# A gated attention layer whose output projection takes seven products: one group's token sums and another group's output products take other places in the order

## The chip, the cores and the metric

The kernel runs on one core of a Trainium2 chip. The metric is the device time of one execution in microseconds (us); lower is better. Several runs are made and their median is taken.

Five engines work side by side, each on its own queue of instructions, in the order in which the program has put them: TensorE (PE in the profile, PEld for its weight loads), VectorE (DVE), ScalarE (ACT), GpSimd (POOL) and SyncE (SP), which here only issues DMAs. Engines wait for one another through semaphores.

## What is computed

`x` and `ctx` are 64 x 128 x 512 in float32; all products are in float32. Cut to what matters:

```python
def xattn(x, k, v):                      # 4 heads of 128
    Q, K, V = heads(x) @ Wh, heads(k) @ Wh, heads(v) @ Wh
    masked = (Q K^T / sqrt(128)) * decay
    A = maximum(abs(masked.sum(over the batch)), 1)     # one A for all 64 sequences
    Y = layernorm(A @ V) * gamma + beta
    return (relu(x @ wg) * Y) @ wo

def ffn(x):                              # inner width 1408
    return ((silu(x @ gate.T * gate_s) * (x @ up.T * up_s)) @ down.T) * down_s

x = x + tanh(g_xattn) * xattn(layernorm(x), ctx, ctx)
x = x + tanh(g_ffn) * ffn(layernorm(x))
```

`A` needs the scores of all 64 sequences, so there are two passes: the first computes the scores and the gates `relu(x @ wg)`, the second everything else.

## The kernel before, in words

The 64 sequences are worked on in 16 groups of four (512 tokens). Products by `wg`, `wo`, `gate`, `up` and `down` are done as products of halves with seven products instead of eight; the price is sums of weights, made once, and sums of tokens, made for each group.

**First pass** (L637 to L670, a loop over groups). For group g:

- `prepare` (L522): for each of the four sequences, statistics on VectorE (`bn`, L251, with two instructions: bn_stats and an aggregate), `inv_std` (L245: an addition `ve` on VectorE, then a power on GpSimd, L249), the normalised tokens `xn` on VectorE (L281), a transpose `pt` on TensorE through an identity (L260), and a copy of `pt` to `xnT`, on VectorE (L552) for odd sequences and on ScalarE (L554) for even ones. For g = 0 the power is made for each sequence by itself, for later groups once for four.
- `scores` (L558) of the group before: products `pq` and `sv`, copies by ScalarE, and additions to `attn` on VectorE (L592, L594).
- `project` (L597) of the group before: first the four token sums `t` of `combine_b` (L322) on VectorE, each of 128 x 512 from the tile `xnT`; then the seven products into the banks a, f, b and c of PSUM, each of four matmuls of 128 x 256, with copies and sums between them.

`gate_weights` (L378) makes the four sums of the `wg` halves on GpSimd, once, when group 1 is prepared. `sum_wo` (L413) scales `down_s` (`ds`, `minus_ds`) and `wo` (`wo_raw`) on VectorE and makes the sums of `wo` on GpSimd; `prepare_weights` (L489) runs it as the first of the weight preparations that are spread over the groups.

**Second pass** (from L676 on). For each group: `retention` (L697) computes `A @ V` (products `po`), statistics and the product with the gate; `attended` (L768) computes the output projection in seven products (`wo_product`, L777) into the tiles bx, bz and by, adds them to `x_t` (L791), and then makes the second layernorm; `ffn` (L912) does the rest. `attended` first makes four sums `ys` (`combine_a`, L328), then yields after each product. While `ffn` of one group runs, `retention` and `attended` of later groups are woven into it: `interleave` (L100) takes steps of several generators in turn, in proportion to the number of steps that it is told for each. For the second group (g = 1) the attention runs beside `ffn` of group 0, in `late_attended` (L1110), which yields nine times, takes the sums, yields three times more and then goes through the products.

**What sets the order.** The program is traced in the order of the Python code, and a scheduler then orders the instructions of each engine by priority and readiness. `tc.issue_after(ins)` puts the instructions of its block behind `ins` where both are on the same engine. The kernel keeps such marks in small lists: `last_norm` (the last `xn`), `last_copy` (the last VectorE copy of `pt`), `last_product` (the last matmul of a `product`, L289), `last_down` (the last matmul of the down projection, L1062). In the version before, the statistics of group 1 are put behind the last copy of group 0, those of later groups behind the last `xn` (L644), and the first output product of a group is put behind the last matmul of the down projection, or behind the last `product` where there was none (L800).

Of the kernel before, what the change touches and what calls it, by code (L numbers as in the profile page):

```python
# [12 lines left out]
ALU = mybir.AluOpType  # L13
# [13 lines left out]
DB11, DB21, DB22, DT1, DT2, DT3, DT4 = range(7)  # L27
# [99 lines left out]
def flamingo_gated_layer(  # L127
# [21 lines left out]
    nc = tc.nc  # L149
    P = 128  # L150
    B, S, DIM = x.shape
# [5 lines left out]
    NG = B // GB  # L157
# [16 lines left out]
    ps_mm = ctx.enter_context(tc.tile_pool(name="ps_mm", bufs=3, space=PSUM))  # L174
    ps_bank = ctx.enter_context(tc.tile_pool(name="ps_bank", bufs=1, space=PSUM))

    last_ve, last_copy = [None], [None]
    last_load, last_norm, last_power, last_product = [None], [None], [None], [None]
    last_down, mid_down = [None], [None]

# [57 lines left out]
    for seeded in (bank_b, bank_c0, bank_c1):  # L238
        for i in range(TOK // P):
            last_seed = nc.tensor.matmul(  # L240
                seeded[:, i * P : (i + 1) * P], lhsT=ident, rhs=ident,
                start=(i == 0), stop=True, skip_group_check=True,
# [79 lines left out]
    def combine_b(engine, t, b11, b12, b21, b22):  # L322
        for dst, in0, in1 in (
            (t[0], b12, b11), (t[1], b22, t[0]), (t[2], b22, b12), (t[3], b21, t[1]),
        ):
            engine.tensor_tensor(dst, in0, in1, ALU.subtract)

    def combine_a(engine, s, a11, a12, a21, a22):  # L328
        engine.tensor_tensor(s[0], a21, a22, ALU.add)
# [34 lines left out]
    tanh_g = const.tile([P, 2], F32, name="tanh_g")  # L364
# [5 lines left out]
    for h in range(H):  # L370
        with tc.issue_after(last_seed.ins):
            nc.tensor.matmul(
                pg[:, h, :], lhsT=whT_sb[:, h, :], rhs=whT_sb[:, h, :],
                start=True, stop=True,
# [37 lines left out]

    def sum_wo(raw):  # L413

        nc.vector.tensor_scalar_mul(ds, ds, tanh_g[:, 1:2])
        nc.vector.tensor_scalar_mul(minus_ds, ds, -1.0)
        nc.vector.tensor_scalar_mul(raw, raw, tanh_g[:, 0:1])
        t = once.tile([P, 4, KC, HN], F32, tag="sums", name="wo_t")
        b = (
            raw[:, 0:KC, 0:HN], raw[:, 0:KC, HN:DIM], raw[:, KC:NC, 0:HN], raw[:, KC:NC, HN:DIM],  # L420
        )
        combine_b(nc.gpsimd, [t[:, i] for i in range(4)], *b)
        return [
            (wo_scr[m], src)
            for m, src in zip(range(7), (b[0], b[2], b[3], t[:, 0], t[:, 1], t[:, 2], t[:, 3]))
        ]
# [95 lines left out]
    def prepare(g, x_t, xnT):  # L522

        n = GB if g else 1

        def statistics(j):
            bn(mean_var[:, g * GB + j, :], x_t[j // 2][:, j % 2, :])
            if (j + 1) % n == 0:
                cols = slice(g * GB + j + 1 - n, g * GB + j + 1)
                inv_std(rstd[:, cols], mean_var[:, cols, 1], LN_EPS, n)  # L530

        def next_statistics(j):

            if g == 0 and j < GB:
                with tc.issue_after((last_norm[0] or last_ve[0]).ins):
                    statistics(j)

        for j in range(1 if g == 0 else GB):
            statistics(j)
        next_statistics(1)  # L540
        yield
        for j in range(GB):
            b = g * GB + j
            with ExitStack() as order:
                if g == 0:
                    order.enter_context(tc.issue_after(last_ve[0].ins))
                xn = normalised(
                    x_t[j // 2][:, j % 2, :], mean_var[:, b, 0:1], rstd[:, b : b + 1]
                )
            pt = transposed(xn, "pt")  # L550
            if j % 2:
                last_copy[0] = nc.vector.tensor_copy(xnT[:, :, j * S : (j + 1) * S], pt)  # L552
            else:
                nc.scalar.copy(xnT[:, :, j * S : (j + 1) * S], pt)  # L554
            next_statistics(j + 2)
            yield
# [40 lines left out]
    def project(g, xnT):  # L597

        b11, b12, b21, b22 = as_b(xnT)
        t = once.tile([P, 4, KC, HT], F32, tag="t1", name="t1")  # L600
        combine_b(nc.vector, [t[:, i] for i in range(4)], b11, b12, b21, b22)
        w = once.tile([P, 2, 2, TOK], F32, tag="w1", name="w1")
        m5 = att.tile([P, TOK], F32, tag="m1", name="m5p")
        bank_c = bank_c0
        product(bank_a, wgc[:, GA11], b11, True)
        nc.scalar.copy(bank_c, bank_a)
        yield
        product(bank_f, wgc[:, GS1], t[:, 0], True)
        nc.scalar.copy(m5, bank_f)
        yield  # L610
        product(bank_a, wgc[:, GA12], b21, False)
        nc.scalar.activation(w[:, 0, 0, :], bank_a, AF.Relu)
        yield
        product(bank_c, wgc[:, GS2], t[:, 1], False)
        nc.scalar.copy(bank_b, bank_c)
        yield
        product(bank_c, wgc[:, GS3], t[:, 2], False)
        nc.vector.tensor_add(w[:, 1, 1, :], bank_c, m5)
        yield
        product(bank_b, wgc[:, GS4], b22, False)  # L620
        nc.vector.tensor_add(w[:, 1, 0, :], bank_b, m5)
        nc.scalar.activation(w[:, 1], w[:, 1], AF.Relu)
        yield
        product(bank_c, wgc[:, GA22], t[:, 3], False)
        relu = nc.scalar.activation(w[:, 0, 1, :], bank_c, AF.Relu)
        if g == NG - 1:

            with tc.issue_after(relu.ins):
                sil = stat.tile([P, 1], F32, tag="rs", name="first_sil")
                nc.scalar.activation(sil, zeros[:, 0:1], AF.Silu)  # L630
        for q in range(2):
            nc.scalar.dma_start(out=w_scr[g, q], in_=w[:, q])
        yield

    pending = None
    weights = prepare_weights()
    first_power = [None]  # L637
    for g in range(NG):
        x_t, c_t = x_next.pop(0), c_next
        xnT = wide.tile([P, NC, TOK], F32, tag="xT", name="xnT")  # L640
        prep = prepare(g, x_t, xnT)
        if g:

            with tc.issue_after((last_copy if g == 1 else last_norm)[0].ins):  # L644
                next(prep)
        else:
            next(prep)
        if g == 1:

            with tc.issue_after(first_power[0].ins):  # L650
                gate_weights()
            constants()
        elif g > 1:

            with tc.issue_after(last_load[0].ins), tc.issue_after(last_power[0].ins):
                next(weights, None)
        held = project(pending[0], pending[2]) if pending else None

        steps = 0 if g == NG - 1 else 7
        interleave(  # L660
            (prep, GB),
            (scores(*pending) if pending else None, 2 + H),
            (islice(held, steps) if pending and steps else None, steps),
        )
        x_next.append(load_x((g + 2) % NG))
        if g + 1 < NG:
            c_next = load_ctx(g + 1)
        pending = (g, c_t, xnT)
        if g == 0:
            first_power[0] = last_power[0]  # L670
# [97 lines left out]
    def attended(g, x_t, ws, x1nT):  # L768
# [6 lines left out]
        yield  # L775

        def wo_product(bank, m, lhs, start):  # L777
            w = att.tile([P, KC, HN], F32, tag="wo", name="wo_w", bufs=3)
            nc.sync.dma_start(out=w, in_=wo_scr[m])
            for i in range(2):  # L780
                for k in range(KC):
                    nc.tensor.matmul(  # L782
                        bank[:, i * HN : (i + 1) * HN],
                        lhsT=lhs[:, k, i * P : (i + 1) * P],
                        rhs=w[:, k, :],
                        start=(start and i == 0 and k == 0),
                        stop=(i == 1 and k == KC - 1),
                        skip_group_check=True,
                    )
# [4 lines left out]

        d1, d2 = slice(0, HN), slice(HN, DIM)
        bx = ps_mm.tile([P, TOK], F32, tag="mm", name="bx")
        if g == 0:
            wo_product(bx, DB11, a11, True)
        else:
            with tc.issue_after((last_down[0] or last_product[0]).ins):  # L800
                wo_product(bx, DB11, a11, True)
        m1 = att.tile([P, TOK], F32, tag="m1", name="m1")
        nc.scalar.copy(m1, bx)  # L803
        for q, d in ((0, d2), (1, d2), (1, d1)):
# [305 lines left out]
    def late_attended(g, x_t, x1nT):  # L1110
        for _ in range(9):
            yield
        steps = attended(g, x_t, ws, x1nT)
        next(steps)
        for _ in range(3):
            yield
        yield from steps

    pending = (0, x_t, x1nT, combine_tokens(nc.vector, x1nT))
    for g in range(NG - 1):  # L1120
        x_t = x_next.pop(0)
        x1nT = new_x1nT()
        if g + 2 < NG:
            x_next.append(load_x(g + 2))
        steps = [attended(g + 1, x_t, ws, x1nT)] if g else [second]
        n_steps = ATT_STEPS + RET_STEPS
        if g == 0:
            steps.append(late_attended(1, x_t, x1nT))
            n_steps += RET_STEPS - 4 + 5
        if g + 2 < NG:  # L1130
            steps.append(next_retention(g + 2))
        interleave(
            (ffn(*pending), FFN_STEPS), (chain(*steps), int(n_steps * 1.4)),
        )
        with tc.issue_after(mid_down[0].ins):
            tokens = combine_tokens(nc.vector, x1nT)
        pending = (g + 1, x_t, x1nT, tokens)
# [59 lines left out]
```

## Time and profile before

| | |
|---|---|
| median of 3 runs | 2223.5 us (2223.39 to 2224.55) |
| the profiled execution | 2223.54 us |
| its span, from the first to the last instruction in the trace | 2221.7 us |
| TensorE busy | 2210.0 us (99%) |
| VectorE, ScalarE, GpSimd busy | 53%, 29%, 29% |
| TensorE clock granted | 1.00 on average |
| first pass | up to about 376 us |

The idle times of TensorE can be counted on two hands, in us from the start of the span: 1.82 ahead of the first matmul, 1.16 at 7.8 and 0.93 at 9.6 (group 0's transposes), 0.57 at 17.2, 0.84 at 19.7, 0.23 at 401, 0.10 at 416, 0.55 at 422, 0.57 at 425, 1.55 at 463, 0.32 at 500, and 3.0 behind the last matmul.

How to read it: a line of a timeline gives the start, the time taken, the engine, the line of the program, the operation, what it writes and what it reads, the shape and how many such instructions are merged. An idle time of the engine just ahead of it stands in brackets with what ended it. A matmul of the program shows as two or more of the profile's records, and their ends are modelled, so a product's length is better taken from one start to the next. A line of a table of stretches gives the stretch, its length, then the busy time of TensorE, its weight loads, VectorE, ScalarE and GpSimd, then the granted TensorE clock (1.00 is full), the share of time in which the DMA engines were busy, and GB/s. The page names the line where a helper issues an instruction, so L326 is any token sum and L281 any normalised tile.

### The profile page before, as it was taken

How to read it: one execution, taken by the hardware profiler on the slowest of the kernel's cores; microseconds unless marked ns; L12 is line 12 of the kernel's file. 1: busy time of each engine (PE TensorE's matmuls, PEld its weight loads, DVE VectorE, ACT ScalarE, POOL GpSimd, SP SyncE). 2: the span in 40 equal slices, each digit the busy share in tenths (PEclk: the TensorE clock that was granted, in tenths of full speed). 3: DMA queues.
4: the chain of work that ended last, by engine and by line, in shares of the span. 5: the costliest groups of instructions: out<-in, count | busy, mean ns of one | idle time of the engine just before them, and what ended most of it. 6: DMA issues, size and time to landing. Idle time of an engine off the chain costs nothing.

```text
span 2221.7 us, 28775 instructions
## 1 busy us (share of the span) xinstructions
PE 2210.0 (99%) x10112; PEld 1889.1 (85%) x10112; DVE 1176.9 (53%) x2866; ACT 642.8 (29%) x1242; POOL 646.3 (29%) x1007
## 2 busy tenths in 40 slices
PE   9999999999999999999999999999999999999999
PEld 7878887788888888888888888888888888888888
DVE  6445554656555555554546464636464646464624
ACT  3444444332222222222222222222222222231221
POOL 2223530241323232323233333333333323241020
PEclk9999999999999999999999999999999999999999
DMA  9886776678686878786878777787777777766654
GB/s 307 268 302 248 259 256 236 242 236 291 242 284 225 285 235 273 236 275 234 274 240 271 250 259 262 251 268 245 261 244 264 244 265 245 268 224 233 229 180 146
DMA packets 217104, 558.47 MB, mean 251 GB/s; under 512 B 21120, under 2 KB 63616, under 8 KB 200192
## 3 DMA queue, kind: packets, MB, share of 16 engines
q1 hardware_dynamic: 211536, 539.58, 72.3%
q10 hardware_dynamic: 5424, 17.04, 1.9%
q8 instruction: 81, 1.33, 0.2%
q14 instruction: 63, 0.52, 0.1%
HBM read 454.31 MB, written 102.24 MB: 251 GB/s over the span
## 4 chain that ended last, share of the span: by engine, by line
PE 98%; DVE 1%; DMA 0%; POOL 0%; issue 0%; ACT 0%; SPq 0%; ACTq 0%; POOLq 0%
PE bank_c L289 22%; PE bank_a L289 15%; PE bank_c L1062 9%; PE bank_b L289 7%; PE bank_f L289 7%; PE bank_b L1062 6%; PE sv L578 5%; PE bank_a L1062 4%; PE bank_f L1062 4%; PE by L782 4%; PE bz L782 3%; PE pq L563 2%; PE bx L782 2%; PE po L704 2%; PE bank_c L942 2%; PE pt L260 1%
## 5 line engine op out<-in xcount | busy, mean ns | idle before, releaser
L289 PE MATMUL bank_c<-tcomb,gu 128*128 128x256 f32 x1920 | 455.0, 380 | 0.3 <-DVE ve L248 0.3
L289 PEld LDWEIGHTS bank_c<-tcomb,gu 128*128 128x128 f32 x1920 | 363.3, 190 | 59.2 <-issue 7.2
L337 POOL TENSOR_TENSOR h<-h 128x128 f32<-128x128 f32 x540 | 243.5, 480 | 400.4 <-DVE h L932 284.2
L289 PE MATMUL bank_a<-x1nT,gu 128*128 128x256 f32 x1280 | 303.1, 379 | 0.6 <-ACT sil L957 0.6
L289 PEld LDWEIGHTS bank_a<-x1nT,gu 128*128 128x128 f32 x1280 | 242.4, 190 | 46.7 <-issue 13.4
L1062 PE MATMUL bank_c<-dn_w,h 128*128 128x256 f32 x896 | 212.0, 379 | 0.0
L1062 PEld LDWEIGHTS bank_c<-dn_w,h 128*128 128x128 f32 x896 | 170.1, 190 | 23.5 <-ACT bank_c L1042 0.2
L931 ACT ACTIVATE sil<-c,gs_sb 128x256 f32<-128x256 f32 x176 | 89.4, 508 | 332.1 <-DVE c L1021 172.3
L337 DVE TENSOR_TENSOR h<-h 128x128 f32<-128x128 f32 x644 | 161.1, 307 | 4.6
L1021 DVE TENSOR_TENSOR c<-bank_c,m 128x512 f32<-128x512 f32 x80 | 55.2, 690 | 202.1 <-PE bank_c L289 200.7
L793 POOL TENSOR_TENSOR x_t<-x_t,m 128x512 f32<-128x512 f32 x48 | 62.1, 1322 | 344.4 <-ACT m L803 320.8
L763 POOL TENSOR_TENSOR w_t<-w_t,yT 128x256 f32<-128x256 f32 x108 | 88.8, 853 | 243.1 <-ACT yT L754 243.1
L249 POOL TENSOR_TENSOR rs<-ve,mhalf 128x1 f32<-128x1 f32 x128 | 73.4, 585 | 294.1 <-DVE ve L248 224.8
L1062 PE MATMUL bank_b<-dn_w,h 128*128 128x256 f32 x640 | 156.4, 379 | 0.0
L289 PE MATMUL bank_f<-tcomb,gu 128*128 128x256 f32 x640 | 151.2, 379 | 0.0
L289 PE MATMUL bank_b<-x1nT,gu 128*128 128x256 f32 x640 | 151.2, 379 | 0.0
L289 PEld LDWEIGHTS bank_b<-x1nT,gu 128*128 128x128 f32 x640 | 121.6, 190 | 22.1 <-issue 6.2
L289 PEld LDWEIGHTS bank_f<-tcomb,gu 128*128 128x128 f32 x640 | 121.6, 190 | 16.5
L1062 PEld LDWEIGHTS bank_b<-dn_w,h 128*128 128x128 f32 x640 | 121.6, 190 | 16.5
L1082 DVE TENSOR_TENSOR x_t<-x_t,bank_c 128x256 f32<-128x256 f32 x192 | 77.7, 419 | 87.4 <-PE bank_c L1062 87.4
L951 ACT COPY bank_c<-bank_a 128x256 f32<-128x256 f32 x16 | 5.7, 357 | 400.2 <-PE bank_a L942 400.2
L578 PE MATMUL sv<-qw,c_t 128*128 128x256 f32 x512 | 120.5, 379 | 0.0
(153 smaller groups left out, 3362.7 us busy)
## 6 DMA issues: line engine op xcount, KB each, us to landing
dn_w<-dn_scr SPq DMA_DIRECT2D x320, 384.0 KB, 4.9
gu<-gu_scr SPq DMA_DIRECT2D x80, 1024.0 KB, 7.8
gu<-gu_scr SPq DMA_DIRECT2D x80, 768.0 KB, 6.2
x_t<-in_x_dram SPq DMA_DIRECT2D x62, 512.0 KB, 5.7
sq_scr<-sq SPq DMA_DIRECT2D x30, 1024.0 KB, 4.8
wo_w<-wo_scr SPq DMA_DIRECT2D x112, 256.0 KB, 3.8
dn_w<-dn_scr SPq DMA_DIRECT2D x96, 256.0 KB, 5.0
c_t<-in_ctxT_dram SPq DMA_DIRECT2D x64, 256.0 KB, 5.9
```

The costliest lines, as they stand in the source:

```text
L249: last_power[0] = nc.gpsimd.tensor_tensor(dst, ve, mhalf[:, :n], ALU.pow)
L289: last_product[0] = nc.tensor.matmul(out, lhsT=w[:, s, k, :], rhs=x_k, start=(start and s == 0 and k == 0), stop=(s == 1 and k == KC - 1), ...
L337: engine.tensor_tensor(slots[to], slots[a], slots[b], ALU.add if sign == "+" else ALU.subtract)
L563: nc.tensor.matmul(pq, lhsT=gram[:, h, :], rhs=xnT[:, h, :], start=True, stop=True)
L578: nc.tensor.matmul(sv[:, 0 : 2 + i : 1 + i, :], lhsT=c_t[j][:, h, :], rhs=qw[:, h, j : GB + 1 : GB - j, :], start=(i == 0), stop=(i == 1), ...
L763: (helper if d or g == 1 else nc.gpsimd).tensor_tensor(w, w, yT[:, :, d * KC + k, q * 2 : q * 2 + 2, :], ALU.mult)
L782: nc.tensor.matmul(bank[:, i * HN : (i + 1) * HN], lhsT=lhs[:, k, i * P : (i + 1) * P], rhs=w[:, k, :], start=(start and i == 0 and k == 0 ...
L793: engine.tensor_tensor(dst, dst, src.rearrange("p (b d) -> p b d", b=2), ALU.add)
L931: nc.scalar.activation(sil, gate, AF.Silu, scale=gs_sb[:, i : i + 1])
L1021: nc.vector.tensor_add(c22, bank_c, m5)
L1062: last_down[0] = nc.tensor.matmul(places[acc], lhsT=hq[q][:, a, :], rhs=dn[n][:, q, :], start=start, stop=True, skip_group_check=True,)
L1082: add = nc.vector.tensor_tensor(dst, dst, places[acc], ALU.add if sign > 0 else ALU.subtract)
```

## The change

In the first pass, for g = 1, `project` of group 0 is started (`next(held)`) before `prepare` of group 1 takes its first step, so that the token sums and the first product are traced first; and the statistics of group 1 are put behind the last of these sums instead of behind the last copy. `combine_b` returns its last instruction for that. The three VectorE instructions of `sum_wo` are put behind the last `xn`.

In the second pass every output product of groups after the first is put behind the last `product` matmul, where before only the first one of a group was put behind the last matmul of the down projection. `late_attended` yields five times instead of three between the sums and the second part, and the number of steps told to `interleave` grows by four.

```diff
-    last_ve, last_copy = [None], [None]
+    last_ve, last_sum = [None], [None]
...
@@ combine_b
-            engine.tensor_tensor(dst, in0, in1, ALU.subtract)
+            last = engine.tensor_tensor(dst, in0, in1, ALU.subtract)
+        return last
...
@@ sum_wo
-        nc.vector.tensor_scalar_mul(ds, ds, tanh_g[:, 1:2])
-        nc.vector.tensor_scalar_mul(minus_ds, ds, -1.0)
-        nc.vector.tensor_scalar_mul(raw, raw, tanh_g[:, 0:1])
+        with tc.issue_after(last_norm[0].ins):
+            nc.vector.tensor_scalar_mul(ds, ds, tanh_g[:, 1:2])
+            nc.vector.tensor_scalar_mul(minus_ds, ds, -1.0)
+            nc.vector.tensor_scalar_mul(raw, raw, tanh_g[:, 0:1])
...
@@ prepare
-                last_copy[0] = nc.vector.tensor_copy(xnT[:, :, j * S : (j + 1) * S], pt)
+                nc.vector.tensor_copy(xnT[:, :, j * S : (j + 1) * S], pt)
...
@@ project
-        combine_b(nc.vector, [t[:, i] for i in range(4)], b11, b12, b21, b22)
+        last_sum[0] = combine_b(nc.vector, [t[:, i] for i in range(4)], b11, b12, b21, b22)
...
@@ the loop of the first pass
         prep = prepare(g, x_t, xnT)
+        held = project(pending[0], pending[2]) if pending else None
+
+        steps = 0 if g == NG - 1 else 7
+        if g == 1:
+
+            next(held)
+            steps -= 1
         if g:
 
-            with tc.issue_after((last_copy if g == 1 else last_norm)[0].ins):
+            with tc.issue_after((last_sum if g == 1 else last_norm)[0].ins):
                 next(prep)
...
-        held = project(pending[0], pending[2]) if pending else None
-
-        steps = 0 if g == NG - 1 else 7
...
@@ attended
         def wo_product(bank, m, lhs, start):
+            if g:
+
+                with tc.issue_after(last_product[0].ins):
+                    return wo_matmuls(bank, m, lhs, start)
+            return wo_matmuls(bank, m, lhs, start)
+
+        def wo_matmuls(bank, m, lhs, start):
             w = att.tile([P, KC, HN], F32, tag="wo", name="wo_w", bufs=3)
...
-        if g == 0:
-            wo_product(bx, DB11, a11, True)
-        else:
-            with tc.issue_after((last_down[0] or last_product[0]).ins):
-                wo_product(bx, DB11, a11, True)
+        wo_product(bx, DB11, a11, True)
...
@@ late_attended
-        for _ in range(3):
+        for _ in range(5):
             yield
...
@@ the loop of the second pass
-            n_steps += RET_STEPS - 4 + 5
+            n_steps += RET_STEPS - 4 + 9
```

## The prediction

> **What bounds the kernel now.** I read the page first (engines' busy shares, chain that ended last), then who waited for whom on TensorE, then the timelines of TensorE, VectorE and GpSimd at the two places the change touches.
>
> ```profile
> PE 2210.0 (99%) x10112; PEld 1889.1 (85%) x10112; DVE 1176.9 (53%) x2866; ACT 642.8 (29%) x1242; POOL 646.3 (29%) x1007
> ...
> PE 98%; DVE 1%; DMA 0%; POOL 0%; issue 0%; ACT 0%; SPq 0%; ACTq 0%; POOLq 0%
> ```
>
> TensorE (PE) is busy 2210.0 of 2221.7 us. The change removes no matmul, so it can give back only part of the 11.7 us of idle time. About 3.0 of those lie behind the last matmul and 1.8 ahead of the first. The waits, longest first (us in total, times, longest):
>
> ```profile
> PE pt L260 <- DVE xn L281: 2.9, 3, 1.2
> ...
> PE bz L782 <- DVE ys L329: 1.6, 1, 1.6
> PE bank_f L289 <- DVE mean_var L254: 0.6, 1, 0.6
> ...
> PE bank_c L289 <- DVE ve L248: 0.3, 1, 0.3
> ```
>
> The first edit aims at the third line and part of the first (0.57 and 0.84 us near 18 and 20 us), the second at the lines of bz and bank_c (1.55 us at 463, 0.32 us at 500). All four together are 3.28 us.
>
> **First edit: token sums ahead of the statistics.** TensorE, then VectorE (DVE), then GpSimd (POOL), in order of time (start, us taken):
>
> ```profile
> 15.32 1.89 PE L289 MATMUL bank_a<-xnT,wgc 128*128 128x256 f32 x8
> 17.78 1.97 PE L289 MATMUL bank_f<-t,wgc 128*128 128x256 f32 x8 [0.57 <-DVE mean_var L254]
> 20.58 0.63 PE L260 MATMUL pt<-ident,xn 128*128 128x128 f32 x4 [0.84 <-DVE xn L281]
> ```
>
> ```profile
> 12.69 0.69 DVE L552 COPY xnT<-pt 128x512 f32<-128x512 f32 x1 [1.22 <-PE pt L260]
> ...
> 16.75 0.88 DVE L326 TENSOR_TENSOR t<-xnT 128x512 f32<-128x512 f32 x1
> 17.56 0.17 DVE L254 BATCH_NORM_AGGREGATE mean_var<-st 128x2 f32<-128x6 f32 x1
> 17.65 0.65 DVE L326 TENSOR_TENSOR t<-xnT 128x512 f32<-128x512 f32 x1
> ```
>
> ```profile
> 13.24 1.27 POOL L331 TENSOR_TENSOR wgc<-wgc 128x512 f32<-128x512 f32 x1
> 14.47 1.27 POOL L330 TENSOR_TENSOR wgc<-wgc 128x512 f32<-128x512 f32 x1
> 15.82 1.27 POOL L332 TENSOR_TENSOR wgc<-wgc 128x512 f32<-128x512 f32 x1
> ```
>
> The built order of the changed kernel puts the four sums t directly behind the copy that ends at 13.38, then the whole of group 1's statistics. On TensorE bank_f's product moves ahead of bank_a's second half, and half of a bank_c product (two matmuls, 0.86 us) moves ahead of the transpose pt. So bank_f no longer waits. TensorE issues a product in 1.73 us and would reach pt at 15.32 + 1.73 + 1.73 + 0.86 = 19.64, ready to go. Since 0.86 us more work lies behind it, pt breaks even at 20.58 + 0.86 = 21.44.
>
> When does pt get its operand xn? That hangs on what the sums cost beside GpSimd's four sums of gate weights (12.02 to 17.09), whose place does not change. The sum at 16.75 took 0.88 instead of 0.65 and ended 0.54 after GpSimd's instruction. At 100 us the same is seen unmixed, one attn sum before and one beside GpSimd's weight sums:
>
> ```profile
> 100.98 0.42 DVE L594 TENSOR_TENSOR attn<-attn,both 128x256 f32<-128x256 f32 x1 [0.75 <-ACT both L586]
> 101.85 1.01 DVE L594 TENSOR_TENSOR attn<-attn,both 128x256 f32<-128x256 f32 x1 [0.44 <-ACT both L586]
> ```
>
> ```profile
> 101.31 1.26 POOL L329 TENSOR_TENSOR gu_raw<-gu_raw 128x512 f32<-128x512 f32 x1
> 102.53 1.46 POOL L331 TENSOR_TENSOR gu_raw<-gu_raw 128x512 f32<-128x512 f32 x1
> ```
>
> The second attn starts at 101.85, GpSimd's instruction ends at 102.57, attn ends 0.29 later, and GpSimd's next one takes 0.20 longer. So such a VectorE sum stands until GpSimd's running instruction is over, then goes, and GpSimd's next one stands meanwhile: they alternate. For 512 columns the price to GpSimd is about 0.45 (at 231.88 a dn_t sum of 0.72 took 1.17 behind a 512-column t).
>
> Step by step: t0 is issued at 13.42, waits until 14.51, ends 15.05 (bank_f at 15.32 is just served). GpSimd's next sum now ends at 14.47 + 1.27 + 0.45 = 16.19, so the second t ends 16.73. GpSimd's last starts 16.27 and ends near 17.94, the third t 18.48 (bank_c's two matmuls at 18.78 are just served). The fourth runs free to 19.2. The statistics then start near 19.12; from the first bn_stats to ve takes 2.85 (27.07 to 29.92), ve to the end of GpSimd's power 1.26 (29.92 to 31.18), and xn to pt 0.69 (19.89 to 20.58), with 0.03 between: 23.95. That is **2.51 us later than break-even**. Without any standing the sums would issue in 0.60, 0.60, 0.73, 0.60 and pt come at 20.78, 0.66 earlier than break-even. Ends: -0.66 and +2.51; I take +2.51, since every sum of this kind beside GpSimd that I looked at stands.
>
> **The clock.** TensorE would then be idle from 19.81 to 23.95, 4.1 us. No gap of before between matmuls is over 1.6 us, so I bound this by the two ends of the run. After the last matmul (ended 2218.67) the granted clock (the column after the engines) falls:
>
> ```profile
> 2218.50:2219.00 0.50, 0.17 (x1) 0.00 (x0) 0.30 (x1) 0.00 (x0) 0.00 (x0) 1.00 0.00 0
> ...
> 2220.50:2221.00 0.50, 0.00 (x0) 0.00 (x0) 0.00 (x0) 0.00 (x0) 0.00 (x0) 0.72 0.04 16
> 2221.00:2221.50 0.50, 0.00 (x0) 0.00 (x0) 0.00 (x0) 0.00 (x0) 0.00 (x0) 0.50 0.00 0
> ```
>
> 0.72 over half a microsecond means half clock from 2220.72 on, 2.05 us after the last matmul. At the start the seeding matmuls are issued 0.21 us apart from 1.82 and 0.11 apart from about 5.4: 3.6 us of work at half rate until it comes back, a loss of at most 1.8. If the clock falls 2.05 us into the gap, some 2.1 of these 3.6 us are idle anyway and the loss is 0.8; if it falls at the gap's end, 1.8. Ends 0 and 3.1 (1.3 and another full stretch); I take the middle, **+1.3**.
>
> The Trainium skill (page "TensorE: Matmul & The Clock Gate", section "Part 1: The HAM clock gate") speaks against this change, but more mildly: it has the clock halved only after at least one whole idle window of about 3.4 us, which runs freely. By that, as an estimate, a 4.1 us gap holds such a window in about a fifth of the phases, and the sum would mostly stay at 2225.9. The fall after 2.05 us in this trace says that less is enough.
>
> **The constants that move.** ds, minus_ds and the scaling of wo_raw (0.48, 0.43, 1.29 on VectorE) go behind group 2's last xn, from 25 and 36 us to about 51. Where they stood VectorE waited 3.2 and 4.1 us for their loads with xnT copies and a w sum behind them, but TensorE has no idle time from 20.6 to 401: no gain. Where they go, ve of group 3 comes at 53.5 instead of 51.7 and GpSimd's power ends near 54.8; xn starts at 55.30 anyhow, and its transpose at 58.39. GpSimd's wo_t sums start 2 us later, and their stores only at 67.30. SP's queue is the same there. I cost it at nothing; without that slack of 2.5 us it would be up to 2 us.
>
> **Second edit: products pinned.** In the built order, everything from bx at 459 to the sixth product of group 1 is unchanged, on VectorE too, so the 1.55 us at bz stay. What moves: the last by one matmul (0.43 us) ahead, the second po one product earlier and with it the fourth, and on SP one load of w_t ahead of one of dn_w, which is needed 40 us later. The bank_c product that waited at 500.74 stands four matmuls (1.73 us) earlier.
>
> ```profile
> 493.73 1.29 DVE L253 BATCH_NORM_STATS2 st<-o 128x6 f32<-128x512 f32 x2 [5.38 <-ACT o L710]
> ...
> 500.03 0.65 DVE L1021 TENSOR_TENSOR c<-bank_c,m 128x512 f32<-128x512 f32 x1
> ```
>
> It waits for the sum at 500.03, behind statistics that wait for the copy of the fourth po. That po goes from 492.06 to 490.34, so the sum should be done at 498.97 and the product start at 499.03, again 0.5 us after TensorE is ready at 498.53. Further on the bank_c product of 504.82, which waits for ScalarE's copy, comes at 504.65: **-0.17**. Ends: -0.5 if the wait goes, +1.7 if VectorE's chain does not come earlier.
>
> **Sum.** The profiled execution took 2223.54 (span 2221.7 and 1.84 around it; the median of the runs is 2223.5, the same). 2223.54 + 2.51 + 1.3 - 0.17 = **2227.2**, a chance of 0.50 (its own range 2226.4 to 2228.2).
>
> **Rivals.**
> 1. The sums stand, the clock stays full: 2225.9. For it: the 1.6 us gaps left the clock alone. 0.16.
> 2. The sums do not stand, the first edit works: 2223.54 - 0.66 - 0.17 = 2222.7. Against it: the attn rows. 0.14.
> 3. **Slower by over 0.2%**: the clock, once down, stays down for a second stretch, because the first is half idle and does not count as busy: 1.3 + 1.8 = 3.1, so 2229.0. It decides if TensorE works less than about half of the first stretch. 0.14.
> 4. The copy of the fourth po gains nothing, and the bank_c product waits 1.7 longer: 2227.2 + 1.9 = 2229.1. 0.04.
> 5. The change does what it says, all four waits go: 2223.54 - 3.28 = 2220.3. The order speaks against it. 0.02.
>
> **Chances.** 0.2% (about what a measurement of this kernel can tell from no change) is 4.4 us: 2219.1 and 2227.9. Slower: rivals 3 and 4 and the upper quarter of my forecast's case, 0.14 + 0.04 + 0.12 = 0.30. Faster: 0.02 for what I have not seen. Same: 0.68. The range 2224.8 to 2229.4 leaves out rivals 2 and 5, 0.16.
>
> **What would show it.** After: bank_f without a wait at 15.3; three of the four sums t at 1.6 to 1.8 us, with GpSimd's weight sums between them; pt with an idle time of about 4 us at 24; matmuls 0.4 us apart instead of 0.2 behind it; granted clock under 1.00 in that slice; bz still waiting 1.5 us. If the four t take 0.65 each, rival 2 is right; if the gap is there and the clock 1.00, rival 1. Wrong altogether would be idle time at a place where the order did not change.

## The result, and the profile after

The changed kernel takes 2227.66 us in the median of 19 runs (2226.69 to 2228.66), against 2223.7 in 19 runs of the kernel before on the same chip; the ratio is 1.0017, 95% interval 1.001 to 1.0024. Two of the 19 runs before took 2977.61 and 7528.47 and stand far from all others. The change makes the kernel about 4 us slower: the interval leaves out 1, and each run of the changed kernel is slower than each of the other 17 before (2223.32 to 2224.55). It is a little less than the 0.2% up to which the forecast speaks of "same". The profiled execution took 2226.98, with a span of 2225.2. The last matmul ends at 2222.18 instead of 2218.66, 3.5 later; the time around the span is the same to within 0.1.

The busy times, and who waited for whom on TensorE (us in total, times, longest):

```profile
PE 2211.2 (99%) x10112; PEld 1891.6 (85%) x10112; DVE 1181.4 (53%) x2866; ACT 643.3 (29%) x1242; POOL 647.1 (29%) x1007
```

```profile
PE pt L260 <- DVE xn L281: 5.8, 3, 4.0
...
PE bz L795 <- DVE ys L330: 1.5, 1, 1.5
...
PE bank_c L289 <- DVE ve L248: 0.3, 1, 0.3
```

Of the four waits that the change could have removed, only that of bank_f is gone. Those of bz and bank_c are as long as before, and the one of pt has grown from 0.84 to 4.0. VectorE's busy time has risen by 4.5 us with the same number of instructions: some of them take longer.

TensorE, VectorE and GpSimd of the changed kernel around this wait (start, us taken):

```profile
15.43 1.89 PE L289 MATMUL bank_f<-t,wgc 128*128 128x256 f32 x8
...
18.89 1.03 PE L289 MATMUL bank_c<-t,wgc 128*128 128x256 f32 x4
23.93 1.09 PE L260 MATMUL pt<-ident,xn 128*128 128x128 f32 x4 [4.02 <-DVE xn L281]
24.81 2.87 PE L565 MATMUL pq<-xnT,gram 128*128 128x512 f32 x4
```

```profile
13.60 3.16 DVE L326 TENSOR_TENSOR t<-xnT 128x512 f32<-128x512 f32 x2
16.68 2.48 DVE L326 TENSOR_TENSOR t<-xnT,t 128x512 f32<-128x512 f32 x2
19.08 1.28 DVE L253 BATCH_NORM_STATS2 st<-x_t 128x6 f32<-128x512 f32 x2
```

```profile
13.27 1.26 POOL L332 TENSOR_TENSOR wgc<-wgc 128x512 f32<-128x512 f32 x1
14.49 1.72 POOL L331 TENSOR_TENSOR wgc<-wgc 128x512 f32<-128x512 f32 x1
16.29 1.60 POOL L333 TENSOR_TENSOR wgc<-wgc 128x512 f32<-128x512 f32 x1
```

The four sums t take 5.6 us together where four by themselves would take about 2.6. They alternate with GpSimd's sums of weights, which are stretched too (1.72 and 1.60 instead of 1.27). Only then do the statistics start, and pt comes at 23.93. Behind the gap pt and pq are issued at half the rate.

The granted clock (the column after the five busy times) in three stretches of 3.41 us shows it:

```profile
19.96:23.37 3.41, 0.00 (x0) 0.00 (x0) 2.24 (x9) 0.00 (x0) 1.02 (x1) 1.00 1.05 386
23.37:26.78 3.41, 2.85 (x7) 1.85 (x8) 1.42 (x3) 0.61 (x2) 0.00 (x0) 0.50 1.03 239
26.78:30.20 3.42, 3.42 (x17) 2.63 (x17) 2.05 (x4) 1.95 (x4) 0.00 (x0) 1.00 0.85 245
```

TensorE is idle in the whole of the first stretch, the clock is 0.50 in the whole of the second, and full again in the third. In the second TensorE works 2.85 us at half rate, so 1.4 us are lost.

**The account of the 3.5 us**, from starts of the same instructions in both traces. The sv behind pt and the waiting bz, before and then after:

```profile
23.20 1.89 PE L578 MATMUL sv<-qw,c_t 128*128 128x256 f32 x8
465.05 1.99 PE L782 MATMUL bz<-wo_w,ys 128*128 128x256 f32 x8 [1.55 <-DVE ys L329]
```

```profile
27.95 1.89 PE L580 MATMUL sv<-qw,c_t 128*128 128x256 f32 x8
468.73 1.99 PE L795 MATMUL bz<-wo_w,ys 128*128 128x256 f32 x8 [1.54 <-DVE ys L330]
```

pt came at 23.93, where 20.58 + 0.86 (the work now ahead of it) + 0.11 (this execution's later start) = 21.55 would have been even: +2.38, and +0.11 for the start. From pt to the next sv takes 4.02 instead of 2.62: +1.40. Small waits around 26 us are gone: -0.21, so bz comes 3.68 later (468.73 instead of 465.05). From bz to the end: -0.17.

### The profile page after: what moved, and what is told of

Read it like the earlier page. It is cut to its first block, busy times and chain, and to the rows that moved or that the text cites. A ratio compares the mean times of both kernels' runs of the same rounds, so it can differ in the third digit from the quotient of the medians.

```text
span 2225.2 us, 28775 instructions
## 1 busy us (share of the span) xinstructions
PE 2211.2 (99%) x10112; PEld 1891.6 (85%) x10112; DVE 1181.4 (53%) x2866; ACT 643.3 (29%) x1242; POOL 647.1 (29%) x1007
## 4 chain that ended last, share of the span: by engine, by line
PE 98%; DVE 1%; DMA 1%; issue 0%; POOL 0%; ACT 0%; SPq 0%; ACTq 0%; DVEq 0%
PE bank_c L289 22%; PE bank_a L289 15%; PE bank_c L1071 9%; PE bank_b L289 7%; PE bank_f L289 7%; PE bank_b L1071 6%; PE sv L580 5%; PE bank_f L1071 4%; PE bank_a L1071 4%; PE by L795 4%; PE bz L795 3%; PE pq L565 2%; PE bx L795 2%; PE po L710 2%; PE bank_c L951 2%; PE pt L260 1%
## 5 line engine op out<-in xcount | busy, mean ns | idle before, releaser
L1030 DVE TENSOR_TENSOR c<-bank_c,m 128x512 f32<-128x512 f32 x80 | 55.3, 691 | 201.9 <-PE bank_c L289 200.5
```

The source lines that it names most:

```text
L1030: nc.vector.tensor_add(c22, bank_c, m5)
```

## The experiments

Two runs of one and the same kernel can differ by up to three microseconds (before: 2223.3 to 2226.4 in 33 runs), so where less is in question the starts of the same instructions in two traces are compared, and the medians stand beside them.

### One part at a time

The first edit alone: the diff shown above without the lines in `sum_wo`, `attended` (`wo_product`), `late_attended` and the second pass's loop.

> The kernel before with the first edit alone: group 0's four sums t and their products stand ahead of group 1's statistics; the constants and the output products are as before. My theory (the sums stand beside GpSimd's weight sums, the transpose pt of group 1 comes at about 23.9, the clock is halved for 3.4 us): three of the four sums take 1.6 to 1.8 us, TensorE's gap ahead of pt is about 4.0 us, and the time is 0.17 above the changed kernel's, about 2227.8, 3.9 to 4.1 above before. Rival (the loss lies in the constants that moved, or in the output products, and not here): pt comes at about 20.8 and the time is that of before to within 1 us.

Measured: 2227.79 (11 runs; before, on the same chip, 2224.26 in 33; ratio 1.0018, 1.0009 to 1.0026). pt came at 23.59 behind a gap of 4.20, with sums of up to 1.75 us. From bz (469.66) to the last matmul's end nothing is won against before (both +4.6). So the whole loss lies in the first edit; the rival is out. The profiled execution showed something more, told below: its clock was down for two stretches.

The second edit alone: the lines of `wo_product`, `late_attended` (3 to 5) and `n_steps` (5 to 9).

> The kernel before with the second edit alone: the output products of group 1 pinned to their places. My theory: the waits at bz (1.5 us) and at the bank_c product (0.3 us) stay, the later bank_c product that waits for ScalarE's copy comes 0.17 earlier, and that is all: -0.17 us in the profiled span, the time within 0.5 us of before. Rival (the pins do what they are for, and the changed kernel lost more elsewhere than I accounted): both waits go and the span is 1.5 to 1.9 us shorter than before. Rival the other way (a pin holds something up): TensorE shows a new wait between 450 and 510 us and the span is longer by its length.

Measured: 2224.35 (11 runs; ratio 1.0001, 0.9992 to 1.001). The waits at bz (1.55) and bank_c (0.32) are there as before. bz starts 0.21 later than before, because bank_f waited 1.25 instead of 0.57 near the start of this run, and the last matmul ends 0.06 later: 0.15 us won in between, as expected, and the median can't show it.

The constants alone:

```diff
-        nc.vector.tensor_scalar_mul(ds, ds, tanh_g[:, 1:2])
...
+        with tc.issue_after(last_norm[0].ins):
+            nc.vector.tensor_scalar_mul(ds, ds, tanh_g[:, 1:2])
...
```

> The kernel before with only the scaling of ds, minus_ds and wo_raw issued behind group 2's last xn. My theory: costs nothing, since TensorE has no idle time from 20.6 to 401 us that hangs on it; TensorE's starts up to 400 us stay the same to within 0.1 us and the time is that of before to within 0.3 us. Rival: the later ve of group 3 (about 2 us) or the later wo_t sums make a wait of up to 2 us on TensorE, and the time goes up by it.

Measured: 2223.59 (11 runs; ratio 1.0, 0.9991 to 1.0008). pt of group 1 comes 0.21 earlier than before (ahead of everything that was moved, so this is a difference between runs), the sv product behind it 0.42 earlier (30.33 instead of 30.75), and it stays so to the end. So the move is not worth nothing, it wins 0.2 us in the trace: before, the sv at 26.75 came 0.09 late, behind the copy of xnT that stood behind VectorE's wait for the load of ds (the copy empties pt, whose buffer sv needs), and the product after it came 0.11 late. The rival's wait does not appear.

### Why the sums take so long

In the changed kernel GpSimd's four sums of gate weights are replaced by fills of the same tiles. The sums of the gate weights are left out.

```diff
-        combine_a(
-            nc.gpsimd, [wgc[:, m] for m in (GS1, GS2, GS3, GS4)],
-            wgc[:, GA11], wgc[:, GA12], wgc[:, 7], wgc[:, GA22],
-        )
+        for m in (GS1, GS3, GS2, GS4):
+            for i in range(3):
+                nc.gpsimd.memset(wgc[:, m], 0.5)
```

> The changed kernel, with GpSimd's four sums of gate weights replaced by twelve fills with a constant on the same tiles: GpSimd is as busy at that place but reads nothing (the gate weights' sums are left out, so the output is not the reference's). My theory (VectorE's sums of two operands stand because GpSimd's running instruction reads two operands too): the four t take about 0.65 each, the statistics start at about 16, the transpose pt comes at about 20.8 with a gap of 1 us or less on TensorE, the clock stays 1.00, and the time is about 2222.7, 4 to 5 us below the changed kernel. Rival (what costs is only that four sums stand ahead, or that GpSimd is busy at all): the four t keep 1.6 to 1.8 us, pt keeps 23.9, and the time stays near 2227.

Measured: 2222.42 (11 runs; before 2223.84 in 27; ratio 0.9993, 0.9985 to 1.0002). VectorE, GpSimd and TensorE of this kernel:

```profile
13.35 1.29 DVE L326 TENSOR_TENSOR t<-xnT 128x512 f32<-128x512 f32 x2
14.56 1.41 DVE L326 TENSOR_TENSOR t<-xnT,t 128x512 f32<-128x512 f32 x2
```

```profile
10.48 5.93 POOL L383 MEMSET wgc<- 128x512 f32 x12
```

```profile
20.73 0.63 PE L260 MATMUL pt<-ident,xn 128*128 128x128 f32 x4 [1.07 <-DVE xn L281]
```

GpSimd is busy from 10.48 to 16.41, over all four sums, but its fills read nothing: two sums take 1.29 instead of 3.16, and pt comes 3.2 us earlier. The clock stays 1.00. So it is shown that VectorE's sums of two operands stand beside GpSimd's sums, which read, and not beside its fills, which only write; that GpSimd is busy at all, or that four sums stand ahead of the statistics, costs little in itself.

### The clock

A pair of kernels: in both, the rest of the bank_c product goes ahead of pt as well (so that the gap is shorter), and in one of them the gap is filled with six matmuls whose sums nothing reads (in the other the range below is 0). For that, the four sums of gate weights are traced ahead of the products in both.

```diff
-            next(held)
-            steps -= 1
+            with tc.issue_after(first_power[0].ins):
+                gate_weights()
+            for _ in range(4):
+                next(held)
+            steps -= 4
+            last_fill[0] = last_product[0]
+            with tc.issue_after(last_product[0].ins):
+                for _ in range(6):
+                    last_fill[0] = nc.tensor.matmul(
+                        bank_c1[:, 0:HT], lhsT=ident, rhs=pending[2][:, 0, 0:HT],
...
+                if g == 1 and j == 0:
+                    order.enter_context(tc.issue_after(last_fill[0].ins))
                 pt = transposed(xn, "pt")
```

> The changed kernel with the rest of that bank_c product (two matmuls more) also ahead of the transpose pt, so that TensorE's gap ahead of pt is shorter by 0.86 us, about 3.2 instead of 4.0, while pt comes at the same time, about 23.9. It is the pair of the kernel with six dummy matmuls in this gap, with the same order otherwise. My theory: the clock still falls about 2 us into the gap or stays down in part; by its phase the half-clock stretch is 0 to 3.4 us long and the time 2225.0 (clock full) to 2226.8 (clock halved). Rival (the clock plays no part in the loss): 2226.8, 0.86 below the changed kernel, whatever the clock shows.

> The same order as its pair without dummies, with six dummy matmuls (whose sums nothing reads) behind the bank_c product ahead of pt, so that TensorE is not idle for more than about 1 us there. pt comes at the same time, about 23.9, since VectorE and GpSimd are untouched. My theory (the idle gap halves the clock, and that costs 1.3 to 1.4 us): the clock stays 1.00 in that stretch and the time is 2225.0 to 2225.4, that is 1.3 to 1.4 below the pair if the pair's clock falls, and the same if it does not. Rival (the clock plays no part): the same time as the pair whatever the pair's clock shows.

Measured: without the dummies 2225.91 (11 runs; ratio 1.0008, 0.9999 to 1.0017), with them 2224.76 (11 runs; ratio 1.0003, 0.9994 to 1.0012). pt stands at 23.71 and 23.72. The gap without dummies was only 2.42 (21.29 to 23.71) and not 3.2, because one matmul of pq (two of the profile's records) went ahead of pt too, in both kernels. Without the dummies, then with them:

```profile
20.27 1.02 PE L568 MATMUL pq<-xnT,gram 128*128 128x512 f32 x2
23.71 0.63 PE L260 MATMUL pt<-ident,xn 128*128 128x128 f32 x4 [2.42 <-DVE xn L281]
```

```profile
19.32 2.75 PE L660 MATMUL bank_c<-xnT,ident 128*128 128x256 f32 x12
23.72 0.63 PE L260 MATMUL pt<-ident,xn 128*128 128x128 f32 x4 [0.79 <-DVE xn L281]
```

The eleven runs without dummies fall in two groups: five with a mean granted clock of 1.000, 2224.71 to 2225.16, and six with 0.999, 2225.91 to 2226.65. With dummies ten of eleven have 1.000, and none takes more than 2225.59, so that the upper six without dummies lie above all of them. The medians of the two groups lie 1.55 apart, and the upper one is 1.6 above the filled kernel, the lower one 0.1. So a gap of 2.4 us appears to halve the clock in about half of the runs, this costs some 1.5 us, and keeping TensorE busy prevents it. The rival (the clock plays no part) is out. That the clock fell in this gap in the upper six is inferred from their mean clock and time; no trace was taken of one.

Both profiled executions were of the kind with the full clock: the first bz, of group 0, starts at 402.72 and 402.71. With a clock that stays up, dummies in a gap are worth nothing.

**The first edit alone again.** Its profiled execution took 1.1 us longer than that of the changed kernel, though pt came 0.34 earlier. Its stretches:

```profile
18.77:22.18 3.41, 0.62 (x3) 0.19 (x2) 2.96 (x10) 0.39 (x1) 0.34 (x1) 1.00 1.05 387
22.19:25.60 3.41, 2.01 (x6) 1.52 (x7) 1.00 (x2) 0.58 (x1) 0.67 (x1) 0.50 0.94 274
25.60:29.00 3.40, 3.40 (x8) 1.74 (x8) 1.30 (x4) 1.17 (x2) 0.00 (x0) 0.50 0.77 176
```

Here the clock fell at 22.18, 1.4 us ahead of pt. The next stretch was busy for 2.01 of 3.41 us, and the clock stayed down for another one. TensorE worked 2.01 + 3.40 us at half rate: 2.7 lost instead of 1.4. The difference of 1.3, less 0.34 for the earlier pt, plus 0.17 for the missing second edit, is the 1.1 by which it ended later. This is rival 3 of the prediction.

The changed kernel's own 19 runs fall in two groups as well: nine from 2226.69 to 2227.15, all with a mean clock of 0.999, and ten from 2227.66 to 2228.66, seven of them with 0.998. The medians of the groups lie 1.3 apart, which is the price of one more stretch. For the seven the clocks say that this is it: 6.83 us at half rate take 0.0015 off the mean over 2226 us, and one stretch with the end of the run takes less. The three with 0.999 can't have had two stretches; what made them late is open (runs of the kernel before scatter as much). The one profile taken is of the lower group.

### The other way round: the sums behind the statistics

If the loss comes from the sums' place beside GpSimd, they can go behind group 1's statistics instead. This kernel has the second edit, and in `project`, in place of the first:

```diff
-        combine_b(nc.vector, [t[:, i] for i in range(4)], b11, b12, b21, b22)
+        with ExitStack() as order:
+            if g == 0:
+                order.enter_context(tc.issue_after(last_ve[0].ins))
+            combine_b(nc.vector, [t[:, i] for i in range(4)], b11, b12, b21, b22)
```

> The second edit as in the changed kernel, and the opposite of the first: group 0's four sums t are issued behind group 1's first statistics (behind ve), not ahead of them and not in between. My theory (what costs is that the statistics' chain to pt stands behind sums that stand beside GpSimd): with ve first, ve is done at about 16.9, GpSimd's power behind its weight sums at about 18.1, the first t is done by 17.7, bank_f's product is issued at 17.8 as before, and the transpose pt directly behind it at about 19.5, without a gap: TensorE's wait for xn near 20 us (0.84) goes, the clock stays 1.00, and the time is 2222.3 to 2222.7, about 1.0 below before. Rival (the sums stand wherever they are, and then pt's wait only turns into a longer one of bank_f): bank_f waits 1 us or more, and the time is that of before or above.

Measured: 2223.44 (11 runs; ratio 0.9996, 0.9987 to 1.0005). TensorE, then VectorE:

```profile
17.71 1.97 PE L289 MATMUL bank_f<-t,wgc 128*128 128x256 f32 x8 [0.76 <-DVE t L326]
19.51 0.60 PE L260 MATMUL pt<-ident,xn 128*128 128x128 f32 x4
...
26.45 1.99 PE L578 MATMUL sv<-qw,c_t 128*128 128x256 f32 x8 [0.73 <-DVE xnT L552]
```

```profile
24.85 0.48 DVE L415 TENSOR_SCALAR ds<-ds,tanh_g 128x512 f32<-128x512 f32 x1 [4.11 <-DMA ds<-in_down_s_dram]
25.37 0.43 DVE L416 TENSOR_SCALAR minus_ds<-ds 128x512 f32<-128x512 f32 x1
25.71 0.68 DVE L552 COPY xnT<-pt 128x512 f32<-128x512 f32 x1
```

bank_f and pt come where I had them (17.8 and 19.5), pt without a gap and 1.07 earlier than before (0.26 of it is this run's earlier start: its bank_a product comes at 15.06 instead of 15.32). But the time missed my expectation by about 0.9: sv now waits 0.73 for the copy of xnT, and that copy stands on VectorE behind the scaling of ds, which waits for its load. At 26.45 only 0.30 of the 1.07 is left, hardly more than the start. What had been hidden under TensorE's work before is a new wait once TensorE is earlier. So the third part of the change is added, the scaling of the constants behind the last xn:

> The kernel with the four sums t behind group 1's statistics and the output products pinned, and now the scaling of ds, minus_ds and wo_raw behind group 2's last xn as well. In the profile without this, the transpose pt came at 19.51 without a gap, but VectorE then stood 4.1 us at ds for its load, with a copy of xnT behind it, and TensorE waited 0.73 for that copy at 26.45. My theory (the loads of the constants took back what the earlier pt had won): this wait goes, the span is shorter by 0.7, the last matmul ends at about 2217.6, and the median is about 2222.7, 1.0 to 1.6 below before. Rival (something else holds VectorE there, or the constants do harm at their later place): TensorE waits as long as before somewhere between 20 and 60 us and the time stays at 2223.4.

Measured: 2222.99 (11 runs; before, on the same chip, 2224.48 in 15; ratio 0.9994, 0.9985 to 1.0003). In its trace the copy of xnT follows its transpose and sv goes on without a wait:

```profile
22.37 0.69 DVE L553 COPY xnT<-pt 128x512 f32<-128x512 f32 x1 [1.57 <-PE pt L260]
```

```profile
25.62 1.89 PE L579 MATMUL sv<-qw,c_t 128*128 128x256 f32 x8
```

The last matmul ends at 2217.27, 1.39 earlier than before (0.16 of it from the start of the run). The median lies between 0.7 (against 2223.7) and 1.5 below before, but the interval holds 1: the trace shows where the time is won, and the runs alone don't prove it. It has the lowest median of the kernels here that compute all of it, some 4.7 us below that of the changed kernel.

## Why the prediction was right, and where it wasn't

The forecast was 2227.2, range 2224.8 to 2229.4, with "same" likeliest; 2227.66 came out, and 2226.98 for the profiled execution, on which the sum was built.

- **The four sums stand beside GpSimd's: right, in each step.** Predicted ends 15.05, 16.73, 18.48, 19.2; measured 15.08, 16.76, 18.44, 19.16. Statistics 19.12 and 19.08, pt 23.95 and 23.93. The prices taken from the trace of before carried over: a standing sum was to end 0.54 behind GpSimd's instruction and ended 0.55 behind it three times, and GpSimd's next was to take 0.45 longer and took 0.45 and 0.33 longer. Rival 2 (they don't stand) is what the kernel with the fills shows: 2222.7 expected, 2222.42 measured.
- **The term of the sums, +2.51: 2.38 measured**, and 0.11 more from the run's start, which was no part of it.
- **The clock: the size +1.3 was near (1.40), its reason was wrong.** I had the fall come some 2 us behind the last matmul, because it did so at the end of the run. In the changed kernel it came 3.5 us behind it, at 23.37, and in the kernel with the first edit alone 2.8. What fits all falls is a grid of stretches, told below. So it was luck that the middle between a fall 2.05 us into the gap (0.8) and one at its end (1.8) came so near. By the grid the second stretch, rival 3, is no separate case of 0.14: by the mean clock it came in 7 of the 19 runs, at some 1.3 more. Its condition was too narrow too: TensorE was to work less than about half of the first stretch, but the clock stayed down behind 2.01 of 3.41. The median of 19 runs is one of the seven, and stands 0.5 above the forecast.
- **The skill's rule that was weighed** (at least one idle window before the clock is halved) would have left the sum mostly at 2225.9, and no run of the 19 is under 2226.69. The fall after 2.05 us in the trace of before was rightly held against it. The profile of the changed kernel alone couldn't have told, since a whole stretch was idle in it; that of the first edit alone does, where the clock fell behind a stretch with 0.62 us of matmuls.
- **The constants at nothing: off by 0.2**, to the good side. "TensorE has no idle time from 20.6 to 401" overlooked two delays of about 0.1 us. What was said of their later place held: allowing for the shift of 3.68, ve of group 3 came at 53.4 (predicted 53.5) and its xn at 55.3, as before; this xn took 0.8 us longer there (see the last section), but its transpose still came at 58.39.
- **The second edit, -0.17: -0.17 in all.** At the product of 504.82 only 0.09 of it is there (508.41, which is 504.73 without the shift; predicted 504.65), the rest some 10 us further on. bz waits as before. bank_c's product came at 502.69, which is 499.01 without the shift (predicted 499.03), with the same wait of 0.32 behind the sum c; the page names ve, an instruction beside it.
- **The rivals not met:** 1 (clock full) is seen in five runs of the unfilled kernel, but with its shorter gap; 4 did not occur, the fourth po's copy came earlier with its product; 5 failed as the order had said.

## What to carry to other kernels

Before a short VectorE chain is moved ahead of another, look at what GpSimd does in the new place: sums of two operands and GpSimd's reads took turns here, at 1.7 us a turn instead of 0.65. A gap of TensorE costs more than its length, here 1.4 to 2.7 us more behind a gap of 4 us, so a wait that is moved and joined to another is not the same as two short ones. And an operand that comes earlier only pays until the next wait on the same engine: 0.77 of 1.07 us were given back at a load for which TensorE had waited only 0.1 us before.

## What the runs showed of the hardware

**The clock goes by a grid of 3.413 us.** In every trace the time for which it is full, from its first rise on, is a whole number of such stretches: 5 in the changed kernel (17.07 us from 6.30 to 23.37), 649 in the kernel before (2215.25 us). The half-clock stretches are 1 (3.41) and 2 (6.83) long. The grid lies differently in each run. Whether the clock falls goes with how busy TensorE was in the stretch just over. It stayed full behind a stretch with 1.54 us of matmuls and fell behind one with 1.35; the first is of the kernel without dummies, the second of the end of the run before:

```profile
21.84:25.25 3.41, 1.54 (x7) 1.07 (x8) 1.58 (x4) 0.68 (x3) 1.02 (x1) 1.00 1.12 292
```

```profile
2217.31:2220.71 3.40, 1.35 (x7) 0.85 (x5) 0.42 (x1) 0.00 (x0) 0.00 (x0) 1.00 0.23 77
2220.72:2221.68 0.96, 0.00 (x0) 0.00 (x0) 0.00 (x0) 0.00 (x0) 0.00 (x0) 0.50 0.02 9
```

In the ten traces there is no counterexample: all stretches with 1.54 us or more kept the full clock, all with 1.35 or less lost it (none lay between; the ends of matmuls are modelled, so the border is rough). It came back behind a stretch busy for 2.85, and not behind those busy for 2.01 (first edit alone) and 2.29 (the start of the run with the second edit alone). From this the price of a gap can be estimated: a gap of 4.0 us takes at least 2 us from one of the two stretches that it lies across, whatever the phase, and leaves it at most 1.4, so that the clock should fall in nearly all runs; a gap of 1.55, as at bz, leaves at least 1.86 and lost the clock in none of the traces.

The Trainium skill (page "TensorE: Matmul & The Clock Gate", section "Part 1: The HAM clock gate") gives a window of 3413 ns that runs freely, and these traces agree (17067 ns for five). It also asks for at least one idle window before the clock is halved; the traces disagree, if that means a window without matmuls: 0.62 and 1.35 us of matmuls in 3.41 were still too few.

**VectorE and GpSimd.** A sum of two operands on VectorE stood until GpSimd's running sum ended, and not beside fills (3.16 against 1.29 for two sums). The Trainium skill (page "SBUF — State Buffer", section "SBUF: two separate sides") has the two arbitrate for one pair of ports, held for a whole instruction, and for a VectorE instruction with two inputs only against a GpSimd instruction that reads; both halves are seen here. Sums are not the only ones to stand: in the changed kernel an xn, which reads one tile, took 1.32 instead of 0.54 beside GpSimd's sums of wo:

```profile
58.99 1.32 DVE L281 TENSOR_SCALAR xn<-x_t,mean_var,rstd 128x512 f32<-128x512 f32 x1
```

```profile
58.76 2.67 POOL L326 TENSOR_TENSOR wo_t<-wo_raw 128x512 f32<-128x512 f32 x2
```

**Not settled: the scatter of the kernel before.** The load of x_t ends at a different time in each of five traces: ahead of group 1's statistics VectorE waited for it for 0 us in the trace of before, 0.30 (constants alone), 0.64 and 0.72 (sums behind), and 0.95 (second edit alone), and in the last bank_f waited 1.25 instead of 0.57. That this makes part of the scatter is likely, but was not tested.
